# Bidirectional scan kernel: the products with B and C of both channel halves as one instruction of 2048 columns, delta u of a direction as one tile and one load

## The chip, the cores and the metric

The kernel runs on one core of a Trainium2 chip. The metric is the time of one execution in device microseconds (us). The core has five engines that work side by side, each in the order of its own queue: PE (matrix products into PSUM), DVE (vector work), ACT (activation functions and copies), POOL (vector work on SBUF alone) and SP, which here only issues transfers (DMAs). They wait for each other through semaphores. An engine that waits holds up everything behind that instruction in its queue, and SP does the same with the loads behind a load that can't be issued yet.

## What is computed

The input is eight images of 64 channels by 128 by 128, f32. The first layer runs a state-space model (Mamba) over all rows, both ways, and over all columns, both ways. Cut to one sequence and direction:

```
xz = in_w @ seq                       # 128 channels x, 128 channels z
u = silu(causal_conv(x))
dt, B, C = split(xp_w @ u)            # 4, 16 and 16 rows
delta = softplus(dt_w @ dt + dt_b)
for t:                                # per channel c and state n
    h[c, n] = exp(delta[c, t] * A[c, n]) * h[c, n] + delta[c, t] * u[c, t] * B[n, t]
    y[c, t] = sum over n of h[c, n] * C[n, t]
out = out_w @ ((y + D * u) * silu(z))
```

The mean of the four passes is group-normalized, goes through silu and is added to the input. A second layer (two 3x3 convolutions with batch norms, relu and a residual) follows.

## The kernel before

**Groups.** Four sequences of 128 points are worked on together: 512 columns. A group `n` is such a block of one image in one orientation; there are 8 x 2 x 32 = 512 groups. All of them run in one long stage; the second convolution, of some 1,300 us with the preparations at the start, comes after it.

**Units.** 128 channels by 16 states by 2 directions don't fit the 128 partitions at once. A tile holds 32 channels x 4 states on its partitions and two blocks of 32 channels side by side: 2 x 512 = 1024 columns. Such a piece of work is a unit `r`; a group has 16 (`UN`). Its `half` (r % 2) says which two of the four channel blocks; `ORDER[r]` gives the state group `ng`, the direction `d` and a kind. Two halves of the same `ng` and `d` use the same B and C, and, apart from the T units, they are neighbours in the order: (0, 1), (2, 3), (5, 6), (8, 9), (10, 11), (13, 14).

A unit goes through these steps, each a function of the kernel:

- `decay` (L421, ACT): two exponentials of 512 columns, exp(delta * A), into a PSUM tile `dA0` or `dA1` by half (for T units into an SBUF tile `s`).
- `drive` (L430): delta u times B, into an SBUF tile `s`. Units of kind V do it on DVE with B from PSUM (`pb`, made on PE by `b_rows`, L410); units of kind G on POOL with B loaded into SBUF (`bt`, by `b_tile`, L403). T units get this product from PE instead (`spread`, `turn`).
- `scan` (L453 for d = 0, L455 for d = 1, DVE): the recurrence along time, in place in `s`.
- `weigh` (L460, POOL): `s` times C (`c`, loaded by `c_rows`, L395), in place.
- `add_up` (L476, PE): for two units at a time (r, r + 1, r even), the sum over the 4 states, accumulated in the PSUM tile `yp`. This frees their `s` tiles.

Delta and delta u are written to DRAM (`dd`, L314) and loaded back with every channel on four partitions. That is `replicate` (L381): for one half and one direction it loads a tile `dl` and a tile `du`, 512 KB each.

**Order.** The order of every queue is written out by hand in the loop over `s`: step `s` is unit r of group n. In step r the loop emits, in this order: the decay of the unit after it; for a V unit the `drive` of the unit after it (so `drive(r + 1)` stands ahead of `scan(r)` on DVE); the `drive` of a G unit from `AHEAD` (r in {7, 8, 15, 0}, three units ahead, on POOL ahead of `weigh(r)`); `scan(r)`; `weigh(r)`; at r = 3 the gate of the group before (L483 on DVE, which reads the finished `yp`); the next piece of `prepare` for the group after; and at even r `add_up` of the pair four steps back (`LAG`), so (12, 13) at step 0 and (14, 15) at step 2 of the next group. At step 3 `b_rows` makes the B rows of unit 5, on PE behind the fold of (14, 15).

**Preparing the next group.** `prepare` is a generator; one piece is emitted a step. Steps 1 to 9 make z, the convolution (`cp`, L290), u, delta (softplus on ACT) and delta u (L326 on DVE, step 9), and store `dd`: first the copy `bc` of B and C (L328, ACT) goes to DRAM, then four writes of delta u and four of delta. Step 10 issues the loads of half 0, d = 0; behind them `fetch` issues c of unit 0 and `bt` of unit 2. Step 11 issues half 1, d = 0, step 13 half 1, d = 1 and step 15 half 0, d = 1.

**Buffers.** Pool `unit`: 8 tiles `s` of 1024 columns, for all kinds. Pool `rep`: five `dl`, five `du` (1024 columns each), two `bt`, five `c`. PSUM is full: `dA0`, `dA1`, `pt` (two banks each), `b` and `yp` (one each).

Of the kernel before, what the change touches and what calls it, by code (L numbers as in the profile page):

```python
# [9 lines left out]
F32 = mybir.dt.float32  # L10
# [5 lines left out]
P = 128  # L16
# [3 lines left out]
N = 512  # L20
# [4 lines left out]
NQ = 4  # L25
# [4 lines left out]
LAG = 4  # L30
# [3 lines left out]
ORDER = (  # L34
    (0, 0, "V"), (0, 0, "V"), (1, 0, "G"), (1, 0, "G"), (2, 0, "T"), (0, 1, "V"), (0, 1, "V"), (2, 0, "T"),
    (1, 1, "V"), (1, 1, "V"), (2, 1, "G"), (2, 1, "G"), (3, 0, "T"), (3, 1, "V"), (3, 1, "V"), (3, 0, "T"),
)
# [9 lines left out]
def tile_mamba2d_then_resblock(ctx: ExitStack, tc: tile.TileContext, x, par, gn, p_w, o_w, new_p, bn, cst, out):  # L47
    nc = tc.nc
# [31 lines left out]
    with tc.tile_pool(name="prep", bufs=2) as prep, tc.tile_pool(name="prep_ps", bufs=2, space=PSUM) as prep_ps:  # L80
# [4 lines left out]
        for o, p in enumerate(par):  # L85
# [8 lines left out]
            for d in range(2):  # L94
                for k in range(2):
                    for e in range(2):
                        h = slice(e * C, (e + 1) * C)
# [121 lines left out]
    with ExitStack() as st:  # L219
        big = st.enter_context(tc.tile_pool(name="big", bufs=1))  # L220
        rep = st.enter_context(tc.tile_pool(name="rep", bufs=2))
        unit = st.enter_context(tc.tile_pool(name="unit", bufs=8))
        work = st.enter_context(tc.tile_pool(name="work", bufs=2))
        small = st.enter_context(tc.tile_pool(name="small", bufs=2))
        scratch = st.enter_context(tc.tile_pool(name="scratch", bufs=2, space=DRAM))
# [48 lines left out]
        def prepare(g, before):  # L274


            w = wt[g["o"]]
            yield
            zp = psa.tile([P, N], F32, name="zp", tag="b")
            nc.tensor.matmul(  # L280
                zp.rearrange("p (q t) -> p q t", t=W), w["wz"], g["xs"][0:C, :, PAD : PAD + W], start=True, stop=True
            )
            yield
            g["sz"] = work.tile([P, N], F32, name="sz", bufs=3)
            nc.scalar.copy(g["sz"], zp)
            cp = psm.tile([P, 2, N], F32, name="cp", tag="pt")
            for d in range(2):
                for k in range(2):
                    t = PAD - 2 * k if d == 0 else PAD + 2 * k + 1
                    nc.tensor.matmul(  # L290
                        cp[:, d, :].rearrange("p (q t) -> p q t", t=W), w["wc"][:, d, k, :],
                        g["xs"][:, :, t : t + W], start=k == 0, stop=k == 1,
                    )
                yield
            yield
            u = work.tile([P, 2, N], F32, name="u")
            nc.scalar.activation(u, cp, AF.Silu, bias=w["conv_b"])  # L297
            if before is not None:
                nc.scalar.activation(before["sz"], before["sz"], AF.Silu)
            g["u"] = u  # L300
            yield
            dp = psm.tile([P, 2, N], F32, name="dp", tag="pt")
            for d in range(2):
                nc.tensor.matmul(dp[:, d, :], w["wd"], u[:, d, :], start=True, stop=True)  # L304
            yield
            yield
            nc.scalar.activation(dp, dp, AF.Softplus, bias=w["dt_b"])
            yield
            dd = g["dd"] = scratch.tile([2, 2, 32, NQ, N], F32, name="dd")

            def keep(k, v):

                for q in range(NQ):
                    nc.sync.dma_start(  # L314
                        out=dd[k, :, :, q, :].rearrange("d c t -> c d t"), in_=v[32 * q : 32 * (q + 1)]
                    )


            bp = psa.tile([P, N], F32, name="bp", tag="b")
            for d in range(2):  # L320
                nc.tensor.matmul(
                    bp[2 * NS * d : 2 * NS * (d + 1), :], w["wbc"], u[:, d, :], start=True, stop=True,
                    skip_group_check=True,
                )
            du = work.tile([P, 2, N], F32, name="du", tag="nat")
            nc.vector.tensor_mul(du, dp, u)  # L326
            bc = work.tile([4 * NS, N], F32, name="bc", tag="tok", bufs=3)
            nc.scalar.copy(bc, bp[0 : 4 * NS, :])  # L328
            bd = g["bd"] = scratch.tile([2 * NS, 2, N], F32, name="bd")
            nc.sync.dma_start(out=bd.rearrange("n d t -> d n t"), in_=bc)  # L330
            if before is not None:
                decay(before, 11)
            dl = work.tile([P, 2, N], F32, name="dl", tag="nat")
            nc.scalar.copy(dl, dp)
            for d, edge in enumerate((0, W - 1)):
                nc.scalar.copy(dl[:, d, :].rearrange("p (s t) -> p s t", t=W)[:, :, edge], far)
            keep(1, du)
            keep(0, dl)
            yield

            dt = (shared.pop("pt", None) or psm.tile([P, 2, N], F32, name="dt", tag="pt"))[:, 1, :]
            for q in range(SEQ):
                c = slice(W * q, W * (q + 1))
                nc.tensor.transpose(dt[:, c], du[:, TD, c], ident)
            replicate(g, 0, 0)
            yield
            g["duT"] = work.tile([P, SEQ, P], F32, name="duT", bufs=1)
            nc.scalar.copy(g["duT"].rearrange("p q c -> p (q c)"), dt)
            replicate(g, 1, 0)
            yield  # L350
            yield

            replicate(g, 1, 1)
            bt = psm.tile([P, 2, N], F32, name="btp", tag="pt")[:, 0, 0 : 8 * SEQ]
            for q in range(SEQ):
                nc.tensor.matmul(
                    bt[:, 8 * q : 8 * (q + 1)], u[:, TD, W * q : W * (q + 1)], w["wbc"][:, 4 * TG : 4 * TG + 8],
                    start=True, stop=True,
                )
            yield  # L360
            g["BT"] = work.tile([P, 8 * SEQ], F32, name="BT", bufs=1)
            nc.scalar.copy(g["BT"], bt)
            yield
            replicate(g, 0, 1)
            yield

        def spread(g, ng, q):
# [7 lines left out]

        def replicate(g, half, d):

            for k, what in enumerate(("dl", "du")):
                t = rep.tile([P, 2, N], F32, name=what, bufs=5)
                src = g["dd"][k, d, :, 2 * half : 2 * half + 2, :].rearrange("c q t -> c (q t)")  # L380
                nc.sync.dma_start(  # L381
                    out=t.rearrange("p q t -> p (q t)"), in_=src.unsqueeze(1).to_broadcast([32, 4, 2 * N])
                )
                g[what, half, d] = t

        def where(r):

# [10 lines left out]
        def b_tile(g, r):  # L398

            half, ng, d = where(r)  # L400
            t = rep.tile([P, N], F32, name="bt", bufs=2)
            src = g["bd"][4 * ng : 4 * ng + 4, d, :]
            nc.sync.dma_start(out=t, in_=src.partition_broadcast(32))  # L403
            g["bt", ng, d] = t
# [8 lines left out]
        def decay(g, r):  # L413

            half, ng, d = where(r)
            if ORDER[r][2] == "T":
                dA = g["s", r] = unit.tile([P, 2, N], F32, name="s")
            else:
                dA = g["dA", r] = psa.tile([P, 2, N], F32, name=f"dA{half}")
            for j in range(2):  # L420
                nc.scalar.activation(  # L421
                    dA[:, j, :], g["dl", half, d][:, j, :], AF.Exp, scale=wt[g["o"]]["A"][:, 2 * half + j, ng : ng + 1]
                )

        def drive(g, r):

            half, ng, d = where(r)
            s = unit.tile([P, 2, N], F32, name="s")
            engine, b = (nc.gpsimd, g["bt", ng, d]) if ORDER[r][2] == "G" else (nc.vector, g["pb"])
            engine.tensor_mul(s, g["du", half, d], b.unsqueeze(1).to_broadcast([P, 2, N]))  # L430
            g["s", r] = s

        def turn(g, r):

# [21 lines left out]

        def weigh(g, r):
            half, ng, d = where(r)
            s, c = g["s", r], g["c", ng, d]
            nc.gpsimd.tensor_mul(s, s, c.unsqueeze(1).to_broadcast([P, 2, N]))  # L460

        def skip(g):

# [6 lines left out]
        def add_up(g, r):  # L470

            for half in range(2):
                s = g.pop(("s", r + half))
                for j in range(2):
                    q = 2 * half + j
                    nc.tensor.matmul(  # L476
                        g["yp"][32 * q : 32 * (q + 1), :], fold, s[:, j, :], start=False, stop=r == UN - 2,
                        skip_group_check=True,
                    )
# [102 lines left out]
        UN = 4 * NG  # L582
# [9 lines left out]
            14: [(2, 0)], 15: [(2, 1), (2, 2)], 0: [(2, 3)], 1: [(3, 0)], 2: [(3, 1)], 3: [(3, 2)], 4: [(3, 3)],  # L592
        }

        AHEAD = {15: 3, 0: 3, 7: 3, 8: 3}

        ROWS = {14: 0, 3: 5, 6: 8, 9: 13}

# [6 lines left out]
        total = UN * len(gs)  # L605
# [3 lines left out]
        def at(s):  # L609
            return gs[s // UN], s % UN  # L610
# [5 lines left out]
        with tc.manual_schedule():  # L616
# [13 lines left out]
            for s in range(total + UN):  # L630
# [17 lines left out]
                    decay(*at(s + 1))  # L648
                if r in EARLY and live:
                    decay(this, EARLY[r])  # L650
                if kind == "V" and s + 1 < total:
                    drive(*at(s + 1))
                if r in AHEAD and s + AHEAD[r] < total:
                    drive(*at(s + AHEAD[r]))
# [14 lines left out]
                        spread(g, *k)  # L669
                if r == LAG and live:  # L670
                    skip(this)
                if s % 2 == 0 and LAG <= s < total + LAG:
                    add_up(*at(s - LAG))
                if r == 9 and live:
                    b_rows(this, ROWS[r])
                if r in NORM and n % PER:
# [174 lines left out]
```

## Time and profile before

| | us |
|---|---|
| median of 3 runs | 26,257.85 |
| lowest, highest | 26,257.84, 26,273.53 |
| span of the profiled execution | 26,239.0 |
| time around the span (median less span) | 18.9 |
| busy: POOL, DVE | 24,022.0, 24,018.6 |
| busy: ACT, PE | 22,246.1, 19,212.0 |
| mean busy share of the DMA engines | about 55% |

The span runs from the first to the last instruction of the profiled execution. In a line of the profile's groups stand the source line, the engine, the operation, what it writes and reads, the shape, the number of instructions; then their busy time, the mean ns of one, and the idle time of the engine just before them with what ended it. A timeline line has the start in us, the duration, the engine (SPq: SP's queue, where a transfer is issued), the line and the number of merged instructions; in brackets the idle time before it and its releaser. The records of vector instructions that follow without a gap overlap a little, so their starts stand closer than their durations.

### The profile page before, as it was taken

What the parts mean: (1) busy time and instruction counts of PE and PEld (TensorE: products, weight loads), DVE (VectorE), ACT (ScalarE), POOL (GpSimd) and SP (SyncE); (2) the same over time, 40 slices, a digit from 0 to 9 for tenths busy, and PEclk for the clock granted to TensorE, in tenths of its full rate; (3) what the DMA queues carried; (4) which work ended last, traced back from release to release, by engine and by line L of the source; (5) the groups of instructions that cost most, each with busy time, mean ns of one, the idle gap of its engine ahead of it and who ended that gap; (6) DMA issues with size and microseconds to landing.
All of it is one profiled execution on the core that took longest, in us unless ns stands there. A gap on an engine that the chain in (4) does not pass through costs nothing. (4 is left out here: it accounts for less than half of the span.)

```text
span 26239.0 us, 266043 instructions
## 1 busy us (share of the span) xinstructions
PE 19212.0 (73%) x75308; PEld 7191.5 (27%) x75308; DVE 24018.6 (92%) x14093; ACT 22246.1 (85%) x41390; POOL 24022.0 (92%) x10404
## 2 busy tenths in 40 slices
PE   6777777777777777777777777777777777777776
PEld 2222222222222223222232222222222222222232
DVE  8999999999999999999999999999999999999932
ACT  7888888888888888888888888888888888888842
POOL 7999999999999999999999999999999999999930
PEclk8888888888888888888888888888888888888888
DMA  5555555555555555555555555555555555555545
GB/s 166 173 175 171 176 186 174 178 169 174 190 171 177 169 177 189 170 176 169 184 182 175 172 176 183 177 177 171 175 185 175 175 171 177 186 172 175 172 140 190
DMA packets 2881499, 4604.73 MB, mean 175 GB/s; under 512 B 1055360, under 2 KB 1334032, under 8 KB 2864144
## 3 DMA queue, kind: packets, MB, share of 16 engines
q1 hardware_dynamic: 2859424, 4486.08, 54.9%
q10 hardware_dynamic: 15984, 68.06, 0.9%
q0 software_dynamic: 4608, 33.56, 0.3%
q8 instruction: 596, 9.76, 0.1%
q14 instruction: 887, 7.27, 0.1%
HBM read 3779.98 MB, written 738.98 MB: 172 GB/s over the span
## 5 line engine op out<-in xcount | busy, mean ns | idle before, releaser
L460 POOL TENSOR_TENSOR s<-s,c 128x1024 f32<-128x1024 f32 x8192 | 19201.7, 2372 | 983.2 <-issue 425.0
L421 ACT ACTIVATE dA<-dl,A 128x512 f32<-128x512 f32 x12288 | 8477.0, 690 | 2320.6 <-DVE s L455 1078.2
L455 DVE TENSOR_TENSOR_SCAN s<-dA,s 128x1024 f32<-128x1024 f32 x4096 | 9162.7, 2272 | 39.9 <-ACT dA L421 9.2
L430 DVE TENSOR_TENSOR s<-du,pb 128x1024 f32<-128x1024 f32 x4096 | 4930.2, 1204 | 1131.8 <-PE yp L476 556.0
L372 ACT ACTIVATE X<-duT,BT 128x128 f32<-128x128 f32 x16384 | 5603.1, 504 | 16.6
L430 POOL TENSOR_TENSOR s<-du,bt 128x1024 f32<-128x1024 f32 x2048 | 4841.3, 2364 | 154.7 <-DMA c<-bd 130.4
L410 PE MATMUL pb<-u,wb 128*128 128x512 f32 x4096 | 2776.4, 765 | 3009.8 <-ACT bc L328 2451.0
L476 PE MATMUL yp<-s,fold 128*32 128x512 f32 x32768 | 4932.0, 678 | 7.9 <-POOL s L460 7.7
L453 DVE TENSOR_TENSOR_SCAN s<-s,dA 128x1024 f32<-128x1024 f32 x2048 | 4666.1, 2278 | 52.9 <-PE dA L439 34.5
L453 DVE TENSOR_TENSOR_SCAN s<-dA,s 128x1024 f32<-128x1024 f32 x2048 | 4528.9, 2268 | 4.8 <-POOL s L430 4.1
L439 PE MATMUL dA<-ident,X 128*128 128x128 f32 x16384 | 2489.2, 301 | 783.3 <-DVE s L455 781.0
L290 PE MATMUL cp<-xs,wc 128*128 128x512 f32 x4096 | 2692.9, 792 | 140.5 <-ACT cs L572 139.7
L439 PEld LDWEIGHTS dA<-ident,X 128*128 128x128 f32 x16384 | 2034.7, 155 | 2597.1 <-DVE s L455 1892.9
L421 ACT ACTIVATE s<-dl,A 128x512 f32<-128x512 f32 x4096 | 2702.9, 707 | 0.0
L280 PE MATMUL zp<-xs,wz 64*128 64x512 f32 x1024 | 895.0, 968 | 1706.6 <-DVE s L430 1436.0
L410 PEld LDWEIGHTS pb<-u,wb 128*128 128x128 f32 x4096 | 715.2, 219 | 4487.4 <-ACT bc L328 2915.0
L476 PEld LDWEIGHTS yp<-s,fold 128*32 128x32 f32 x32768 | 824.0, 117 | 3298.8 <-issue 2282.6
L304 PE MATMUL dp<-u,wd 128*128 128x512 f32 x2048 | 1117.8, 672 | 332.7 <-ACT u L297 331.7
L421 ACT ACT_TABLE_LOAD x1030 | 1321.5, 1283 | 18.4
L290 PEld LDWEIGHTS cp<-xs,wc 128*128 128x128 f32 x4096 | 898.2, 243 | 1520.1 <-issue 969.0
L466 PE MATMUL yp<-u,dg 128*128 128x512 f32 x2048 | 961.2, 591 | 1.6 <-DVE y L483 1.6
L789 POOL DMA_DIRECT2D out<-cc x32 | 17.2, 538 | 971.9 <-ACT cc L788 971.9
(118 smaller groups left out, 13940.4 us busy)
## 6 DMA issues: line engine op xcount, KB each, us to landing
dl<-dd SPq DMA_DIRECT2D x2048, 512.0 KB
du<-dd SPq DMA_DIRECT2D x2048, 512.0 KB
c<-bd SPq DMA_DIRECT2D x4096, 256.0 KB
dd<-du SPq DMA_DIRECT2D x2048, 128.0 KB
dd<-dl SPq DMA_DIRECT2D x2048, 128.0 KB
bt<-bd SPq DMA_DIRECT2D x1024, 256.0 KB
xs<-x_h SPq DMA_DIRECT2D x512, 128.0 KB
bd<-bc SPq DMA_DIRECT2D x512, 128.0 KB
```

The costliest lines, as they stand in the source:

```text
L290: nc.tensor.matmul(cp[:, d, :].rearrange("p (q t) -> p q t", t=W), w["wc"][:, d, k, :], g["xs"][:, :, t : t + W], start=k == 0, stop=k == 1,)
L304: nc.tensor.matmul(dp[:, d, :], w["wd"], u[:, d, :], start=True, stop=True)
L372: nc.scalar.activation(t[:, :, n], g["duT"][:, q, :], AF.Copy, scale=g["BT"][:, k : k + 1])
L410: nc.tensor.matmul(pb, wt[g["o"]]["wb"][:, P * ng : P * (ng + 1)], g["u"][:, d, :], start=True, stop=True)
L421: nc.scalar.activation(dA[:, j, :], g["dl", half, d][:, j, :], AF.Exp, scale=wt[g["o"]]["A"][:, 2 * half + j, ng : ng + 1])
L430: engine.tensor_mul(s, g["du", half, d], b.unsqueeze(1).to_broadcast([P, 2, N]))
L439: nc.tensor.transpose(dB[:, j, W * q : W * (q + 1)], g["X", ng, q][:, 32 * (2 * half + j) : 32 * (2 * half + j + 1), :].rearrange("p c n - ...
L453: nc.vector.tensor_tensor_scan(s, a, b, 0.0, ALU.mult, ALU.add)
L455: nc.vector.tensor_tensor_scan(s[:, ::-1], a[:, ::-1], b[:, ::-1], 0.0, ALU.mult, ALU.add)
L460: nc.gpsimd.tensor_mul(s, s, c.unsqueeze(1).to_broadcast([P, 2, N]))
L466: nc.tensor.matmul(g["yp"], wt[g["o"]]["dg"], g["u"][:, d, :], start=d == 0, stop=False, skip_group_check=True)
L476: nc.tensor.matmul(g["yp"][32 * q : 32 * (q + 1), :], fold, s[:, j, :], start=False, stop=r == UN - 2, skip_group_check=True,)
```

## The change

- `drive` makes the product for both halves in one instruction of 4 x 512 = 2048 columns, into a tile `s2` of its own kind; the scans still run on each half (1024 columns).
- `weigh` multiplies both halves by C in one instruction, behind the scan of the second. T units keep theirs of 1024.
- `du` of a direction is one tile of 2048 columns with one load of 1 MB (`replicate_du`): d = 0 at step 10 behind `dl` of half 0, d = 1 at step 15 behind `dl` of half 0. `replicate` loads `dl` alone.
- V products are emitted once a pair, at step r where r + 1 is in `FIRST` = (0, 5, 8, 13); G products from the new `AHEAD`: that of (2, 3) of the next group at step 13 and that of (10, 11) at step 5.
- `add_up` follows the table `FOLD` (the step, and how many units back): (0, 1) at step 5, (2, 3) at 6, (4, 5) at 10, (6, 7) at 11, (8, 9) at 13, (10, 11) at 15, (12, 13) at 1 and (14, 15) at 2 of the next group.
- Buffers: four `s2` of 2048 columns and three `s` of 1024 for T units (before: eight `s`); two `du` of 2048 (five of 1024); one `bt` (two).

```diff
--- before.py
+++ after.py
@@ -219,7 +219,7 @@
     with ExitStack() as st:
         big = st.enter_context(tc.tile_pool(name="big", bufs=1))
         rep = st.enter_context(tc.tile_pool(name="rep", bufs=2))
-        unit = st.enter_context(tc.tile_pool(name="unit", bufs=8))
+        unit = st.enter_context(tc.tile_pool(name="unit", bufs=4))
         work = st.enter_context(tc.tile_pool(name="work", bufs=2))
         small = st.enter_context(tc.tile_pool(name="small", bufs=2))
         scratch = st.enter_context(tc.tile_pool(name="scratch", bufs=2, space=DRAM))
@@ -343,6 +343,7 @@
                 c = slice(W * q, W * (q + 1))
                 nc.tensor.transpose(dt[:, c], du[:, TD, c], ident)
             replicate(g, 0, 0)
+            replicate_du(g, 0)
             yield
             g["duT"] = work.tile([P, SEQ, P], F32, name="duT", bufs=1)
             nc.scalar.copy(g["duT"].rearrange("p q c -> p (q c)"), dt)
@@ -362,6 +363,7 @@
             nc.scalar.copy(g["BT"], bt)
             yield
             replicate(g, 0, 1)
+            replicate_du(g, 1)
             yield
 
         def spread(g, ng, q):
@@ -375,13 +377,19 @@
 
         def replicate(g, half, d):
 
-            for k, what in enumerate(("dl", "du")):
-                t = rep.tile([P, 2, N], F32, name=what, bufs=5)
-                src = g["dd"][k, d, :, 2 * half : 2 * half + 2, :].rearrange("c q t -> c (q t)")
-                nc.sync.dma_start(
-                    out=t.rearrange("p q t -> p (q t)"), in_=src.unsqueeze(1).to_broadcast([32, 4, 2 * N])
-                )
-                g[what, half, d] = t
+            t = g["dl", half, d] = rep.tile([P, 2, N], F32, name="dl", bufs=5)
+            src = g["dd"][0, d, :, 2 * half : 2 * half + 2, :].rearrange("c q t -> c (q t)")
+            nc.sync.dma_start(
+                out=t.rearrange("p q t -> p (q t)"), in_=src.unsqueeze(1).to_broadcast([32, 4, 2 * N])
+            )
+
+        def replicate_du(g, d):
+
+            t = g["du", d] = rep.tile([P, NQ, N], F32, name="du", bufs=2)
+            src = g["dd"][1, d].rearrange("c q t -> c (q t)")
+            nc.sync.dma_start(
+                out=t.rearrange("p q t -> p (q t)"), in_=src.unsqueeze(1).to_broadcast([32, 4, NQ * N])
+            )
 
         def where(r):
 
@@ -398,7 +406,7 @@
         def b_tile(g, r):
 
             half, ng, d = where(r)
-            t = rep.tile([P, N], F32, name="bt", bufs=2)
+            t = rep.tile([P, N], F32, name="bt", bufs=1)
             src = g["bd"][4 * ng : 4 * ng + 4, d, :]
             nc.sync.dma_start(out=t, in_=src.partition_broadcast(32))
             g["bt", ng, d] = t
@@ -414,7 +422,7 @@
 
             half, ng, d = where(r)
             if ORDER[r][2] == "T":
-                dA = g["s", r] = unit.tile([P, 2, N], F32, name="s")
+                dA = g["s", r] = unit.tile([P, 2, N], F32, name="s", bufs=3)
             else:
                 dA = g["dA", r] = psa.tile([P, 2, N], F32, name=f"dA{half}")
             for j in range(2):
@@ -425,10 +433,13 @@
         def drive(g, r):
 
             half, ng, d = where(r)
-            s = unit.tile([P, 2, N], F32, name="s")
+            s = unit.tile([P, NQ, N], F32, name="s2")
             engine, b = (nc.gpsimd, g["bt", ng, d]) if ORDER[r][2] == "G" else (nc.vector, g["pb"])
-            engine.tensor_mul(s, g["du", half, d], b.unsqueeze(1).to_broadcast([P, 2, N]))
-            g["s", r] = s
+            engine.tensor_mul(s, g["du", d], b.unsqueeze(1).to_broadcast([P, NQ, N]))
+            for k in (r, r + 1):
+                h = k % 2
+                g["s", k] = s[:, 2 * h : 2 * h + 2, :]
+            g["s2", r + 1] = s
 
         def turn(g, r):
 
@@ -456,8 +467,14 @@
 
         def weigh(g, r):
             half, ng, d = where(r)
-            s, c = g["s", r], g["c", ng, d]
-            nc.gpsimd.tensor_mul(s, s, c.unsqueeze(1).to_broadcast([P, 2, N]))
+            if ORDER[r][2] == "T":
+                s = g["s", r]
+            elif ("s2", r) in g:
+                s = g.pop(("s2", r))
+            else:
+                return
+            c = g["c", ng, d]
+            nc.gpsimd.tensor_mul(s, s, c.unsqueeze(1).to_broadcast(list(s.shape)))
 
         def skip(g):
 
@@ -592,7 +609,9 @@
             14: [(2, 0)], 15: [(2, 1), (2, 2)], 0: [(2, 3)], 1: [(3, 0)], 2: [(3, 1)], 3: [(3, 2)], 4: [(3, 3)],
         }
 
-        AHEAD = {15: 3, 0: 3, 7: 3, 8: 3}
+        AHEAD = {13: 5, 5: 5}
+        FOLD = {5: 5, 6: 4, 10: 6, 11: 5, 13: 5, 15: 5, 1: 5, 2: 4}
+        FIRST = (0, 5, 8, 13)
 
         ROWS = {14: 0, 3: 5, 6: 8, 9: 13}
 
@@ -648,7 +667,7 @@
                     decay(*at(s + 1))
                 if r in EARLY and live:
                     decay(this, EARLY[r])
-                if kind == "V" and s + 1 < total:
+                if (r + 1) % UN in FIRST and s + 1 < total:
                     drive(*at(s + 1))
                 if r in AHEAD and s + AHEAD[r] < total:
                     drive(*at(s + AHEAD[r]))
@@ -669,8 +688,8 @@
                         spread(g, *k)
                 if r == LAG and live:
                     skip(this)
-                if s % 2 == 0 and LAG <= s < total + LAG:
-                    add_up(*at(s - LAG))
+                if r in FOLD and FOLD[r] <= s < total + FOLD[r]:
+                    add_up(*at(s - FOLD[r]))
                 if r == 9 and live:
                     b_rows(this, ROWS[r])
                 if r in NORM and n % PER:
```

## The prediction

> **What bounds the kernel now.** First the busy shares and the costliest groups. They are read for two things: which engines are full, and what one instruction costs.
>
> ```profile
> PE 19212.0 (73%) x75308; PEld 7191.5 (27%) x75308; DVE 24018.6 (92%) x14093; ACT 22246.1 (85%) x41390; POOL 24022.0 (92%) x10404
> ...
> L460 POOL TENSOR_TENSOR s<-s,c 128x1024 f32<-128x1024 f32 x8192 | 19201.7, 2372 | 983.2 <-issue 425.0
> ...
> L430 DVE TENSOR_TENSOR s<-du,pb 128x1024 f32<-128x1024 f32 x4096 | 4930.2, 1204 | 1131.8 <-PE yp L476 556.0
> ...
> L430 POOL TENSOR_TENSOR s<-du,bt 128x1024 f32<-128x1024 f32 x2048 | 4841.3, 2364 | 154.7 <-DMA c<-bd 130.4
> ```
>
> POOL and DVE are equally full, and DVE's idle time stands almost wholly before L430, its product with B. The list of waits says for what:
>
> ```profile
> DVE s L430 <- PE yp L476: 556.0, 574, 3.8
> DVE s L430 <- DMA du<-dd: 528.5, 570, 14.3
> ```
>
> So about once a group DVE waits for a fold that frees an s buffer, and once for the load of delta u. The timeline of one group shows the loop that closes there. Time is counted from the end of the scan of unit 7 (17.72 + 2.28 = 20.00 after 20,000), called zero below.
>
> ```profile
> 20017.72 2.28 DVE L453 TENSOR_TENSOR_SCAN s<-s,dA 128x1024 f32<-128x1024 f32 x1
> ...
> 20026.51 0.57 ACT L328 COPY bc<-bp 64x512 f32<-64x512 f32 x1
> ...
> 20035.22 0.54 SPq L381 DMA_DIRECT2D dl<-dd  x1
> ...
> 20037.10 0.60 SPq L403 DMA_DIRECT2D bt<-bd  x1
> ...
> 20043.51 2.35 POOL L430 TENSOR_TENSOR s<-du,bt 128x1024 f32<-128x1024 f32 x1
> ...
> 20045.82 2.36 POOL L460 TENSOR_TENSOR s<-s,c 128x1024 f32<-128x1024 f32 x1
> 20046.28 1.22 DVE L430 TENSOR_TENSOR s<-du,pb 128x1024 f32<-128x1024 f32 x1 [1.87 <-DMA du<-dd]
> ```
>
> From unit 7's scan, ACT's softplus work leads to the copy of bc (end 7.1), SP then writes dd and issues the loads (dl half 0 at 15.2), and the first product of the next group that needs du half 1 starts at 26.3. Over 502 groups of the trace the copy ends at 7.1 (7.09 to 7.16 from the 10th to the 90th percentile), so this chain is rigid, and that product starts at 26.0. DVE then needs 22.8 to the next unit 7; 26.0 + 22.8 is the 48.83 us that I find between successive L326 instructions. **This loop (zero, loads, DVE, zero) is the bound**; POOL, at about 47, follows close behind. The execution is 26,239.0: 511 distances of 48.83 are 24,952, and 1,287 lie outside. The median run is 18.9 above the span.
>
> **What is saved.** Where instructions follow without a gap, starts on POOL are 2.32 apart for L460 and 1.22 for the 128x512 addition L528. Another 512 columns thus cost 1.10, and 2048 columns 2.32 + 2.20 = 4.52 against 4.64 for two. Per group six products with C and two with B merge on POOL: 8 x 0.12 = 0.96. On DVE L430 starts are 1.12 apart and L483 with 512 columns 0.58, so 2048 columns cost 2.20 against 2.24; four merges give 0.16. The row of L787, 2048 columns on DVE at 2351 ns busy, bounds this price from above. The saving is POOL's, and POOL isn't the bound. The Trainium skill (GPSIMD Engine Reference, 3.1 Elementwise) gives 4497 ns for a tensor_tensor of 2048 f32 columns, where the rows here (2372 ns, and 1268 ns for 512 columns) make 2372 + 2 x 1104 = 4580 busy; by the page the chain below would be 0.17 us a group shorter, some 85 in all.
>
> **What moves.** Three things, per group:
>
> (1) *Delta u half 1 is loaded sooner, and needed sooner.* The packets' records give these mean ends: dl half 0 at 18.3, du half 0 at 20.8, bt at 21.9, dl half 1 at 23.3, du half 1 at 25.0. The moved bytes of that window, per 0.75 us from 20,030 on:
>
> ```profile
> GB/s 128 161 213 306 249 249 169 5 0 339 202 382 404 366 320 150 306 317 388 407 410 423 410 412 412 432 415 388 404 359 239 208 169 129 33 90 246 14 0 0
> ```
>
> So 512 KB take 1.67 once the queue is full, and the consumer starts 1.0 after the last packet. In the new order du is one load behind dl half 0: 18.3 + 2 x 1.67 = 21.6, usable at 22.6. But its DVE product now stands ahead of the scan of unit 15, not behind it. DVE reaches it at 19.9: scans 8, 9 (4.4), L326 (1.1), a wait to 6.65 for the decay of unit 10 (ACT gives it just before the bc copy, of 0.57, starts), scans 10, 11 (4.4), the product of 13 (2.2), scans 12 to 14 (6.6). So DVE waits 2.7 instead of 0.9. The old 0.93 wait for a fold before the product of 13 (second position after scan 11) goes, and is swallowed by this one.
>
> (2) *POOL's product with B for units 2 and 3 is moved ahead of the products with C of 13, 14 and 15* (AHEAD from 15: 3 to 13: 5). It needs bt of the next group, which SP issues behind dl half 0, the whole of du and c0. These are 0.5 + 1.0 + 0.25 + 0.25 MB = 2.1 MB, exactly what now lies ahead of the end of dl half 1, so bt's last packet is at 23.3 and it is usable at 24.3. POOL has finished unit 12 by about 18 (below). It stands in order, so it **idles some 6 us, and the C products of 13/14 and 15 queue behind**: 24.3 + 4.52 + 4.52 = 33.34 (13/14 done), + 2.32 = 35.66 (15 done; before, POOL finished it at 28.2 in the rows above).
>
> (3) *Who waits for those.* PE's order is written out: the fold of (12, 13) at step 1, the conv product cp at step 2, the fold of (14, 15), then at step 3 pb for unit 5. The DVE gate L483 waits for the last fold, and the DVE product for 5 and 6 for pb. From 33.34: 0.1 to start, fold 1.07 (eight records of L476 in this timeline), cp 1.99 (four of L290 in the group at 13,017; 3.69 in this one, with PE's weight loads 0.34 instead of 0.19), fold 1.07, pb 1.12 (L410), 0.1: DVE starts that product at 38.8. Without this wait it would be there at 22.6 + 2.2 + five scans at 2.2 + gate 0.6 = 36.4. Then 2.2 + scans 4 to 6 (6.6) + 2.2 + scan 7 (2.28) = 13.3. **The new distance is 38.8 + 13.3 = 52.1.**
>
> Check on POOL: from 35.66, units 0/1 to 40.2, 2/3 to 44.7, 4 to 47.0, B of 10/11 to 51.5, that is -0.6 in the next group; 5/6 to 3.9, 7 to 6.3, 8/9 to 10.8, 10/11 to 15.3, 12 to about 18. So it does stand ready long before 24.3.
>
> *Cost nothing by this walk:* bt with one buffer instead of two: its old reader, the B product of 10/11, ends at -0.6, and the new load is issued at 17; without these 17 us of cover every us that POOL lags more would be paid. The Trainium skill (Trainium Kernel Development and Optimization, Best Practices) asks for double buffers so that loads and work overlap, and so speaks against this; the issue at 17.1 shows the overlap kept, and by the rule some of bt's 1 us would be added. Also the four s2 buffers (each reused fold lies at least 3 us back), SP's c load of unit 13 (waits for 5/6 at 3.9; bd is due at 7.1), and ACT (its continuous run of decays and X between scan 0 and scan 6 is 13.1 against 13.8 of DVE). One load issue less in two is about 0.6 of SP, which isn't late.
>
> **Sum.** 52.1 - 48.83 = 3.25 (unrounded); x 511 = 1,661; 26,239 + 1,661 + 19 = **27,920**. Ends: if the queue ran at 410 GB/s, as in the burst's later slices, the 1.57 MB behind dl half 0 would take 3.8 instead of 5.0, so 1.2 a group less: 27,300. If cp always took 3.69, 1.7 more: 28,790; PE's granted clock over the trace is 0.847, so I take a third of it, 28,210, and half of the lag of SP below on top: 28,500.
>
> **Rivals.** *Only the du load decides* (POOL's products of 14, 15 not late enough, or PE not held): 22.6 + 27.1 = 49.7, +0.8 a group: 26,690. For it: the wait for du is in the list already. Against: the 6 us between POOL ready and bt. 14%.
>
> *Faster, the merged instructions count.* If neither load binds, DVE's spaced work is the next floor: 48.83 less its waits of about 2.4 is 46.4, less 0.16 is 46.2; POOL about 46. With 1 us of remaining waits, 47.2, or -1.6 a group: 25,420. One thing decides it: bt must be usable before 48.83 - (52.1 - 24.3) = 21.0, not 24.3, and du before 21.7. That needs 1.57 MB in 1.7 us behind dl half 0; no slice in the burst passes 432 GB/s. It remains for a queue order other than the one I read. 13%.
>
> *Worse.* POOL's lag blocks SP: x1's write waits for POOL in a quarter of the groups, and the c loads in all; if bd starts 1.5 later in every group the distance is 53.6: 28,690. 8%.
>
> *The change doesn't do what it says* (the load of half 1 isn't needed earlier since the tile framework splits it): no more than 0.2% either way, 3%.
>
> **Numbers.** Forecast 62%, own range 27,300 to 28,500. The range 26,600 to 28,700 takes in the du rival and half of the worse one, and leaves out the faster one. What can be told from no change is about 0.2%, or 53 us. Faster 13%, same 3%, slower 84%.
>
> **What would show it.** Right: a gap on POOL of 4 to 7 us before L430, released by the bt load; a gap on DVE before the gate L483 (released by PE's yp) or the product behind it of 2 to 3 us, where all 512 together wait 7.5 us now; a gap before the first product released by du of 2 to 3; L326 distances near 52. POOL's busy time falls by 8 x 0.164 (2 x 2372 less 4580 ns) x 512, some 670 us, while the span grows. Wrong: POOL without that gap, or bt landing at 21 or sooner; then the walk's order of loads is false. If the gap is there but the gate doesn't wait, the step through PE is false, and the time is that of the du rival.

## The result, and the profile after

| | before | after |
|---|---|---|
| median of 4 runs, us | 26,257.85 | 28,919.85 |
| lowest, highest | 26,254.96, 26,273.53 | 28,910.66, 28,929.12 |
| span of the profiled execution | 26,239.0 | 28,927.3 |
| mean distance between the scans of unit 7 | 48.82 | 54.05 |
| mean granted clock of TensorE | 0.847 | 0.812 |

The changed kernel is **slower by a tenth**: ratio 1.1008, interval 1.0992 to 1.1023. I had forecast 27,920: the sign was right, the size too small by 1,000 us, and the time lies above the range. 511 distances of 54.05 are 27,620, and 1,307 lie outside them (1,291 before, by the same measure); so the loss is in the groups, 5.23 us in each.

The busy shares and costliest groups of the changed kernel, the lines that answer to those of before:

```profile
PE 19901.2 (69%) x75308; PEld 7280.4 (25%) x75308; DVE 24040.4 (83%) x12045; ACT 22313.5 (77%) x41390; POOL 23399.6 (81%) x6308
...
L438 POOL TENSOR_TENSOR s<-du,bt 128x2048 f32<-128x2048 f32 x1024 | 4656.0, 4547 | 3217.9 <-DMA bt<-bd 2902.9
...
L438 DVE TENSOR_TENSOR s<-du,pb 128x2048 f32<-128x2048 f32 x2048 | 4659.0, 2275 | 1375.2 <-DMA du<-dd 800.2
```

POOL's work shrank by 622 us in 4,096 fewer instructions, and DVE's not at all (22 us more); POOL now stands still for a fifth of the span and DVE for a sixth. What they stand still for is in the list of waits of the changed kernel (total us, times, longest):

```profile
POOL s L438 <- DMA bt<-bd: 2902.9, 479, 7.6
PE yp L493 <- POOL s L477: 2497.5, 508, 7.5
...
DVE y L500 <- PE yp L493: 1424.2, 461, 5.2
...
DVE s L466 <- ACT dA L429: 816.4, 765, 1.6
DVE s L438 <- DMA du<-dd: 800.2, 297, 14.6
```

The first three lines are one chain: POOL waits for bt once a group (some 6 us), PE then for POOL's product with C, and DVE's gate for PE's fold. Before, the gate waited 7.5 us in all. The timeline of one group of the changed kernel shows it in order of time. Its zero, the end of the scan of unit 7, is 20,010.81.

```profile
20008.53 2.28 DVE L464 TENSOR_TENSOR_SCAN s<-s,dA 128x1024 f32<-128x1024 f32 x1
...
20017.49 4.47 DVE L466 TENSOR_TENSOR_SCAN s<-dA,s 128x1024 f32<-128x1024 f32 x2 [1.21 <-ACT dA L429]
...
20034.58 2.29 DVE L438 TENSOR_TENSOR s<-du,pb 128x2048 f32<-128x2048 f32 x1 [2.30 <-PE pb L418]
20035.95 4.53 POOL L438 TENSOR_TENSOR s<-du,bt 128x2048 f32<-128x2048 f32 x1 [6.99 <-DMA bt<-bd]
...
20040.44 15.87 POOL L477 TENSOR_TENSOR s<-s,c 128x2048 f32<-128x2048 f32 x4
...
20045.03 1.92 PE L493 MATMUL yp<-s,fold 128*32 128x512 f32 x4 [5.97 <-POOL s L477]
...
20046.88 3.23 PE L290 MATMUL cp<-xs,wc 128*128 128x512 f32 x4
...
20050.04 1.07 PE L493 MATMUL yp<-s,fold 128*32 128x512 f32 x8
...
20051.03 1.12 PE L418 MATMUL pb<-u,wb 128*128 128x512 f32 x2
20051.20 0.69 DVE L500 TENSOR_TENSOR y<-yp,sz 128x512 f32<-128x512 f32 x1 [3.29 <-PE yp L493]
...
20052.20 2.29 DVE L438 TENSOR_TENSOR s<-du,pb 128x2048 f32<-128x2048 f32 x1 [0.31 <-PE pb L418]
```

POOL idles 6.99 for bt; the product with C of 13/14 starts at 20,040.44 (29.6 after zero) and ends 4.5 later; PE, idle for 5.97, folds unit 13 and makes cp, and only then comes the fold of (14, 15), for which the gate has waited 3.29. New to the forecast are two durations on PE: after its idle time four records of the fold take 1.92, and cp takes 3.23; the next fold and pb run in 1.07 and 1.12 again.

The same in means over 500 groups, us after zero, with the walk of the prediction beside it:

| | forecast | measured |
|---|---|---|
| POOL's B product of 2/3 starts | 24.3 | 24.24 |
| POOL idle before it | some 6 | 6.05 |
| DVE's product of 0/1 starts | 22.6 | 23.36 |
| PE starts the fold of unit 13 | 33.44 | 33.42 |
| cp starts | 34.5 | 35.26 |
| cp takes | 1.99 | 3.42 |
| fold of (14, 15) ends | 37.6 | 39.73 |
| DVE's product of 5/6 starts | 38.8 | 40.9 |
| distance | 52.1 | 54.05 |

Along the chain from bt over POOL to PE's fold the walk holds within 0.1 us; DVE's product of 0/1 came 0.8 late, which costs nothing here, since the gate waits 3 us later on. **The whole miss of 2 us arises between 33.4 and 39.7, on PE**, and 13.2 from the product of 5/6 to the next zero is again as forecast (13.3).

### The profile page after: what moved, and what is told of

It reads as the page before. It is cut to its first block, busy times and chain, and to the rows that moved or that the text cites. A ratio compares the mean times of both kernels' runs of the same rounds, so it can differ in the third digit from the quotient of the medians.

```text
span 28927.3 us, 254788 instructions
## 1 busy us (share of the span) xinstructions
PE 19901.2 (69%) x75308; PEld 7280.4 (25%) x75308; DVE 24040.4 (83%) x12045; ACT 22313.5 (77%) x41390; POOL 23399.6 (81%) x6308
## 5 line engine op out<-in xcount | busy, mean ns | idle before, releaser
L477 POOL TENSOR_TENSOR s<-s,c 128x2048 f32<-128x2048 f32 (+1 forms) x5120 | 18641.8, 3667 | 1219.5 <-issue 720.9
L493 PE MATMUL yp<-s,fold 128*32 128x512 f32 x32768 | 5973.5, 708 | 2497.5 <-POOL s L477 2497.5
L438 POOL TENSOR_TENSOR s<-du,bt 128x2048 f32<-128x2048 f32 x1024 | 4656.0, 4547 | 3217.9 <-DMA bt<-bd 2902.9
L418 PE MATMUL pb<-u,wb 128*128 128x512 f32 x4096 | 2996.5, 821 | 4155.0 <-ACT bc L328 4144.6
L438 DVE TENSOR_TENSOR s<-du,pb 128x2048 f32<-128x2048 f32 x2048 | 4659.0, 2275 | 1375.2 <-DMA du<-dd 800.2
L450 PE MATMUL dA<-ident,X 128*128 128x128 f32 x16384 | 2361.9, 291 | 217.4 <-DVE s L466 212.0
L500 DVE TENSOR_TENSOR y<-yp,sz 128x512 f32<-128x512 f32 x512 | 354.1, 692 | 1566.9 <-PE yp L493 1424.2
L280 PE MATMUL zp<-xs,wz 64*128 64x512 f32 x1024 | 675.4, 743 | 817.9 <-DVE s L438 722.0
L304 PE MATMUL dp<-u,wd 128*128 128x512 f32 x2048 | 1020.5, 621 | 312.5 <-ACT u L297 312.5
L357 PE MATMUL btp<-xpT,u 128*128 128x8 f32 x4096 | 657.6, 288 | 508.3 <-ACT xp L523 329.3
```

Source lines behind the costliest of these rows:

```text
L280: nc.tensor.matmul(zp.rearrange("p (q t) -> p q t", t=W), w["wz"], g["xs"][0:C, :, PAD : PAD + W], start=True, stop=True)
L418: nc.tensor.matmul(pb, wt[g["o"]]["wb"][:, P * ng : P * (ng + 1)], g["u"][:, d, :], start=True, stop=True)
L438: engine.tensor_mul(s, g["du", d], b.unsqueeze(1).to_broadcast([P, NQ, N]))
L450: nc.tensor.transpose(dB[:, j, W * q : W * (q + 1)], g["X", ng, q][:, 32 * (2 * half + j) : 32 * (2 * half + j + 1), :].rearrange("p c n - ...
L477: nc.gpsimd.tensor_mul(s, s, c.unsqueeze(1).to_broadcast(list(s.shape)))
L493: nc.tensor.matmul(g["yp"][32 * q : 32 * (q + 1), :], fold, s[:, j, :], start=False, stop=r == UN - 2, skip_group_check=True,)
```

## Experiments: the chain from bt over POOL to PE

**Undo the move on POOL.** The product of 2/3 goes back to step 15, behind the products with C of 13/14 that it held up; all else is as in the changed kernel.

```diff
-        AHEAD = {13: 5, 5: 5}
+        AHEAD = {15: 3, 5: 5}
```

> The kernel after with one entry changed: POOL's product with B for units 2 and 3 of the next group is issued at step 15, behind the product with C of 13/14, instead of at step 13 ahead of it. Theory (the chain bt load, POOL's queue, PE's queue, gate): 13/14 no longer waits for bt, 15 ends at 24.3 + 4.5 + 2.3 = 31.1 instead of 35.7, the gate waits no more, and what is left is the loop through the load of du: 23.4 + 27.1 = 50.5 us between groups, 27,100 us in all. Rival 1 (DVE's own waits set the loop, for du 2.4 and for the decay of unit 10 1.2, and the gate's wait is only slack): no change, 28,900. Rival 2 (the 2048-column pieces are too coarse, wherever they stand): above 28,500.

Measured: 27,273.24, ratio 1.0387 (1.0371 to 1.0402), distance 50.83. DVE's waits in this kernel:

```profile
DVE s L466 <- ACT dA L429: 814.4, 764, 1.6
DVE s L438 <- DMA du<-dd: 693.3, 265, 15.5
```

The gate's wait for yp, 1,424 us in the changed kernel, is down to 8, and POOL's gap before the B product of 2/3 fell from 6.05 to 0.05 a group. On top of the rest of the change the move costs 28,920 less 27,273, so **1,647 us, 62% of the loss**. The other 1,010 us belong to the rest of the change. What is left waiting: 1.88 a group before the product of 0/1, 1.21 before scan 10, 0.51 before scan 12, 0.39 before scan 14. The first of these has two causes: in the row groups du ends it (2.5 a group), in the column groups mostly pb on PE (1.2), as in the changed kernel (2.8 and 2.0).

**Leave the move and take cp out of the way**: the fold of (12, 13) goes to step 2, behind cp, so that cp runs while PE would wait.

```diff
-        FOLD = {5: 5, 6: 4, 10: 6, 11: 5, 13: 5, 15: 5, 1: 5, 2: 4}
+        FOLD = {5: 5, 6: 4, 10: 6, 11: 5, 13: 5, 15: 5, 2: 4}
...
+                if r == 2 and 6 <= s < total + 6:
+                    add_up(*at(s - 6))
```

> The kernel after with PE's fold of (12, 13) moved from step 1 to step 2, behind the conv product cp; nothing else. Theory: cp runs before POOL has finished 13/14, so the wait costs only two folds and pb behind 35.7: the gate starts 2 to 3.5 us sooner, 50.7 to 52.1 us between groups, 27,200 to 27,900 us. If PE's queue is not in the chain: 28,900, no change.

Measured: 28,072.38, ratio 1.069 (1.0674 to 1.0706), distance 52.37. The right direction, with less effect than expected. The gate's wait fell from 3.06 to 0.80, but the product behind it now waits 0.70 for pb: the folds end at 37.64, since unit 15's product with C is late too (35.7 by the prediction's walk), and pb stands behind them.

**Leave the order and keep PE busy.** Five f32 products with the identity, whose result nobody reads, stand ahead of the fold of (12, 13); nothing of the computation is left out. In the timeline below each is two records.

```diff
+                if r == 1 and live and n:
+                    wp = psm.tile([P, 2, N], F32, name="wp", tag="pt")
+                    for k in range(5):
+                        nc.tensor.matmul(wp[:, 0, :], ident, this["u"][:, 0, :], start=True, stop=True)
```

> The kernel after with five more f32 matrix products of 512 columns per group into a PSUM tile that nobody reads, on PE just ahead of the fold of (12, 13), where PE stands idle for some 6 us. Theory: PE's granted clock is 0.5 in the stretch after that idle time, so that fold and cp take 1.9 and 3.4 us; with work in the idle time it is granted 1.0, they take 1.1 and 2.0, and the distance falls by about 2 us to 52: 27,900 us. Rival (the slow clock has nothing to do with PE's idling): no gain, or up to 1.5 us a group more, 28,900 to 29,700.

Measured: 28,406.88, ratio 1.0816 (1.0798 to 1.0834), distance 53.04, half of the gain expected. By kind of group, the column groups went from 53.83 to 51.56 and the row groups without a convolution from 54.04 to 51.60. The row groups in which a piece of the second layer's convolution or norm is emitted went up, from 54.41 to 55.59. The loss is in the convolution's 18 of 64 groups (54.06 to 55.83; of the rest all but the first of an image gained): there the idle products wait for the PSUM tile `pt` that this work holds, until ACT has copied it out (502 us in 112 waits). So the products were left out in the convolution's groups:

```diff
-                if r == 1 and live and n:
+                if r == 1 and live and n and not 6 <= n % PER < 24:
```

> As warm, but the five idle products are left out in the 18 of 64 groups in which the first convolution holds the PSUM tile that they use (there warm lost 1.2 us a group, in all others it won 2.3). Theory: 46 groups at 51.6 and 18 at 54.3 us, mean 52.3, 28,000 us. Rival (the loss lies elsewhere): 28,300 or more.

Measured: 28,137.34, ratio 1.0712 (1.0696 to 1.0728), distance 52.51; column groups 51.53, row groups without a convolution 51.58, the others 54.17. The timeline of a group with the idle products (zero is 18,879.67):

```profile
18904.30 4.54 POOL L438 TENSOR_TENSOR s<-du,bt 128x2048 f32<-128x2048 f32 x1 [6.48 <-DMA bt<-bd]
...
18906.99 4.56 PE L694 MATMUL wp<-u,ident 128*128 128x512 f32 x10
...
18911.49 1.05 PE L493 MATMUL yp<-s,fold 128*32 128x512 f32 x4
...
18913.40 1.05 PE L493 MATMUL yp<-s,fold 128*32 128x512 f32 x4 [0.87 <-POOL s L477]
...
18914.39 1.99 PE L290 MATMUL cp<-xs,wc 128*128 128x512 f32 x4
...
18916.31 1.06 PE L493 MATMUL yp<-s,fold 128*32 128x512 f32 x8
...
18917.47 0.69 DVE L500 TENSOR_TENSOR y<-yp,sz 128x512 f32<-128x512 f32 x1 [0.74 <-PE yp L493]
```

POOL waits for bt as before (6.48), and the fold and cp read and write the same data in the same order, but they take 1.05 and 1.99 instead of 1.92 and 3.23. The view by windows says why. First the six us of the changed kernel's group from PE's idle time to the fold, and the six behind it; then the second six for the group with idle products (PE, PEld, DVE, ACT and POOL busy, granted clock, DMA share, GB/s):

```profile
20039.00:20045.00 6.00, 0.06 (x2) 0.00 (x0) 6.00 (x4) 5.80 (x14) 6.00 (x3) 0.80 0.43 178
20045.00:20051.00 6.00, 5.97 (x16) 1.52 (x16) 2.90 (x2) 5.97 (x15) 6.00 (x2) 0.63 0.47 119
```

```profile
18912.00:18918.00 6.00, 5.13 (x22) 1.41 (x19) 5.25 (x4) 5.97 (x16) 6.00 (x3) 1.00 0.22 80
```

PE does nothing for 6 us, and the clock granted in the 6 us behind that is 0.63; where it was kept at work the clock there is 1.00. That settles the 2 us: it is **the clock after an idle PE**, on average 4.9 us idle in the changed kernel.

## Experiments: the parts by themselves

**One load of delta u, nothing else.** The kernel before with `replicate_du` as in the change; B products in halves, the old order.

```diff
+            replicate_du(g, 0)
...
-            engine.tensor_mul(s, g["du", half, d], b.unsqueeze(1).to_broadcast([P, 2, N]))
+            engine.tensor_mul(s, g["du", d][:, 2 * half : 2 * half + 2, :], b.unsqueeze(1).to_broadcast([P, 2, N]))
```

> The kernel before with one part of the change alone: du of a direction as one tile of 2048 columns with one load of 1 MB; the products stay in halves, in their old order. Theory (the loop through the load of du): both halves are usable at 23.4 us after the scan of unit 7 instead of 20.8 + 1.0 and 26.0; the product of unit 0 (at 21.7 before) waits 1.7 us, and that of unit 1 comes at 23.4 + 1.1 + 2.2 = 26.7 instead of 26.0: 49.5 us between groups, 26,600 us. Rival (half as many loads relieve SP and the DMA queue): 26,000 or less.

Measured: 26,269.03, ratio 1.0002 (0.9993 to 1.0011). My expectation was wrong; the load by itself costs nothing and saves nothing. DVE's waits in this kernel:

```profile
DVE s L438 <- PE yp L484: 592.6, 599, 2.4
...
DVE s L438 <- DMA du<-dd: 546.3, 424, 15.6
```

The two totals are close to those of before (556.0 and 528.5). The wait has only moved: the gap before the product of unit 0 grew from 0.24 to 1.17 a group, that before unit 1 fell from 0.88 to nothing, and unit 1's product started at 26.04 as it had at 26.00.

**The merged products with C alone.** The kernel before with `s2` tiles and one `weigh` for both halves; B products in halves, two loads of du; to make room du has four buffers and bt one. `weigh` is that of the change.

```diff
+            if r + 1 < UN and ORDER[r] == ORDER[r + 1] and ("s2", r) not in g:
+                s2 = g["s2", r + 1] = unit.tile([P, NQ, N], F32, name="s2")
+            else:
+                s2 = g["s2", r]
+            s = s2[:, 2 * half : 2 * half + 2, :]
```

> The kernel before with another part of the change alone: the products with C merged to 2048 columns (six a group), everything else in halves as before. To make room, du has four buffers instead of five and bt one instead of two. Theory (POOL is not the bound before the change, the load of du is): POOL's busy time falls by about 500 us, and the time stays within 0.3% of before. Rival (POOL is the bound): 6 x 0.12 = 0.7 us a group less, 25,890 us.

Measured: 26,443.44, ratio 1.0067 (1.0052 to 1.0082), so worse than I allowed. The loss stands in one kind of group: those in which POOL adds x1 (`xr`) went from 49.23 to 50.48, the others from 48.70 to 48.81. Fewer buffers of du and bt came with the merged products here, and no run tells the two apart.

**Undo more from the changed kernel's side.** On top of the move undone, DVE's product of 0/1 goes behind scan 15; then in addition the load of du is issued ahead of `dl`'s.

```diff
-        FIRST = (0, 5, 8, 13)
+        FIRST = (5, 8, 13)
...
+                if r == 0 and live and s:
+                    drive(this, 0)
```

> The kernel of pool15 (POOL's product of units 2/3 at step 15) and DVE's product of units 0/1 moved behind the scan of unit 15, to step 0. Theory (what is left is the loop through du): DVE needs du 2.2 us later and waits some 0.5 us for it; 23.4 + 24.9 = 48.3 us between groups, 25,950 us. Rival (DVE's work and ACT's decays are the floor, not du): as pool15, within 0.5%.

Measured: 26,875.1, ratio 1.0232 (1.0217 to 1.0247), well above what I expected. The wait for du is nearly gone (164 us), and the row groups without a convolution came down from 49.8 to 48.1; but the wait of 1.21 before scan 10 stays, and in the column groups, at 51.1, scan 15 waits 2.10 for `turn` on PE.

```diff
-            replicate(g, 0, 0)
             replicate_du(g, 0)
+            replicate(g, 0, 0)
```

> As pool15_v0, and the load of du (d = 0) is issued ahead of that of dl of half 0 instead of behind it. Theory: du is usable 2 us sooner, at 21.4, and no product waits for it; what is left is DVE's own work and waits on ACT, 46.2 + 1 to 1.5 = 47.2 to 47.7 us between groups, 25,400 to 25,700 us. Rival (dl of half 0, now 3.3 us later, is late for the decay of unit 0): 26,200 or more.

Measured: 26,830.52, ratio 1.0216 (1.0201 to 1.0231). A miss: du no longer decided anything, and the two waits that did are untouched. Some 570 us over the kernel before remain. Why PE's `turn` is late in the column groups I have not settled by a run. The trace of the kernel above shows where: their output takes a second product on PE, `btp` starts at 18.5 us after zero against 16.1 in the row groups without a convolution, the clock granted from 20 to 22 is 0.50 against 1.00, and `turn` starts at 23.0 against 19.0. Their median distance is 51.2 in this kernel, in the one above and in the first experiment.

## Experiments: towards a faster kernel

**The old order, with the parts that cost nothing.** The kernel before with merged C products and one load of du, that of d = 0 issued ahead of `dl`; B products in halves where they were, bt with one buffer.

```diff
+            replicate_du(g, 0)
             replicate(g, 0, 0)
```

> The kernel before with merged products with C and du as one tile and load, that load issued ahead of dl of half 0; the products with B stay in halves, in the old order. Theory: du is usable at 21.4, as the product of unit 0 asks for it at 21.7, so nothing waits for du: 48.8 less 0.9 for du, less some of the 0.9 before the product of unit 13, 47.2 to 48.0 us between groups, 25,400 to 25,850 us. Rival (POOL takes over as the bound at its 46.4): not below 46.8, 25,200; or dl late for the decays: 26,200 or more.

Measured: 26,046.51, ratio 0.9914 (0.9898 to 0.9931): faster, by less than I hoped. What waits most now is scan 12 (0.96 a group), whose `turn` on PE stands behind a fold of (6, 7) that waits for the merged product:

```profile
DVE s L465 <- PE dA L451: 482.6, 480, 1.9
```

So this fold was moved one step, from 10 to 11, behind that `turn`:

```diff
-                if s % 2 == 0 and LAG <= s < total + LAG:
-                    add_up(*at(s - LAG))
+                late = 5 if r == 11 else LAG
+                if (s % 2 == 0 and r != 10 or r == 11) and late <= s < total + late:
+                    add_up(*at(s - late))
```

> As b_both_duf, with PE's fold of (6, 7) moved from step 10 to step 11, behind the transposes that the scan of unit 12 waits for. Theory: the 0.96 us a group that DVE waits before that scan falls to about 0.1, nothing else stands ready to take its place: 48.4 - 0.9 = 47.5 to 47.7 us between groups, 25,570 to 25,670 us. Rival (POOL, at 46.6 busy, or the load of du takes over): 25,900 or more.

Measured: **25,859.17, ratio 0.9845 (0.983 to 0.986)**, the best kernel of this study, faster than before and after. Scan 12's wait is gone, and the time is some 200 us above the expected one: waits of 0.16 to 0.37 a group are left before scans 14, 1, 2 and 3, all but that of scan 3 hardly there before. On this one the two merged B products were put back singly.

**With DVE's B products merged**, at the places of the change:

```diff
+            if ORDER[r][2] == "V":
+                engine.tensor_mul(s2, g["du", d], b.unsqueeze(1).to_broadcast([P, NQ, N]))
...
-                if kind == "V" and s + 1 < total:
+                if (r + 1) % UN in (0, 5, 8, 13) and s + 1 < total:
```

> As b_both_fold11, and DVE's products with B merged to 2048 columns, at the steps of the change (each ahead of the scan of the unit before its pair). Theory: the merge saves 0.16 us a group and costs more, since the product of unit 9 no longer stands between the scans of 7 and 8 while ACT works through softplus: the scan of unit 10 waits 1.2 us; in column groups the scan of 15 or 14 waits too. 1.0 to 1.8 us a group over b_both_fold11, 26,100 to 26,500 us. Rival (only POOL's order did harm): as b_both_fold11 or 0.2 us a group less, 25,500.

Measured: 26,166.12, ratio 0.9962 (0.9947 to 0.9977): 307 us slower than without, as expected. The wait for ACT's decay before scan 10, first without and then with the merged products:

```profile
DVE s L467 <- ACT dA L429: 135.6, 276, 0.8
```

```profile
DVE s L473 <- ACT dA L429: 694.0, 652, 1.6
```

In halves, unit 9's product stands behind scan 7, and covers 1.12 us of ACT's softplus work before decay 10. Merged, it stands ahead of scan 7, and the wait a group rises from 0.09 to 1.21: by 1.12, just that product. DVE's busy time fell by 169 us, and the kernel still grew by 307.

**With POOL's B products merged**, at steps 15 and 7:

```diff
+            if ORDER[r][2] == "G":
+                engine.tensor_mul(s2, g["du", d], b.unsqueeze(1).to_broadcast([P, NQ, N]))
...
-        AHEAD = {15: 3, 0: 3, 7: 3, 8: 3}
+        AHEAD = {15: 3, 7: 3}
```

> As b_both_fold11, and POOL's products with B merged to 2048 columns, at steps 15 (behind the product with C of 13 and 14) and 7. Theory: POOL isn't the bound, so its 0.24 us a group bring nothing; unit 15's product with C comes 2.2 us later, and PE's fold of (14, 15) at step 2 still doesn't wait: within 0.4% of b_both_fold11. Rival (POOL is the bound now): 25,450 us.

Measured: 26,113.55, ratio 0.9941 (0.9925 to 0.9958), 254 us slower than without, where I had expected no difference. All of it is in the groups with an `xr` addition: 48.82 became 51.08, the others stayed at 47.86 and 47.85. In this kernel SP's 128 waits for that addition, before x1 is written, are 2,032 us together, against 1,674 without the merged products, so 2.8 us longer each, and DVE's waits for du rose from 58 to 336 us. That fits a load of du that is queued behind the write; no run took that wait away alone.

## Why the forecast was right in sign and too small

**Right.** The loop through bt, POOL, PE and the gate is what the change puts in place of the old one. Putting POOL's product back took 1,647 us away. Most of the signs that I had named are there: POOL's gap of 6.05 released by bt (4 to 7), the gate's 3.06 (2 to 3), and 2.37 before the product of 0/1 (2 to 3), though du ends it in the row groups only (249 of 256) and in most column groups pb does (204 of 255). The distance, 54.05 and not near 52, is the one that failed. POOL's saving of 622 us (670 forecast) buys nothing, since POOL isn't the bound.

**The step that failed is (3), PE's order, in the durations "fold 1.07, cp 1.99".** Both were read from stretches in which the clock was full. Measured are 33.42 to 35.26 for the fold and 3.42 for cp, 2.2 us more together than forecast. The steps behind gave 0.2 back, and 2 x 511 is the missing 1,000 us. The records of the granted clock, averaged over 490 groups, show it: 0.50 from 33 to 36 us after zero, 0.59 to 0.73 from 36 to 39, 0.99 from 40 on. The idle products in all groups brought the clock from 33 to 38 up to 0.87 to 0.95, cp to 2.01, and the column groups and the row groups without a convolution to 51.5 to 51.6, where I had forecast 52.1. So the mechanism and the rest of the sum stand; the term on PE was mis-sized.

The trace of before could have told me. Over its groups cp took 3.36 on average and 1.99 only in one group of seven; I had both 1.99 and 3.69 in view and chose 1.99 as the rule. Where cp was slow there, PE's longest idle time in the 9 us ahead of it was 3.9 us on average, where it was fast 0.8. The mean alone gives 52.1 + 1.4 and some 28,600, inside the range. And for the range I weighed 3.69 with the clock over the whole trace, 0.847; the clock where cp runs, 28 to 32 us after zero, was 0.62 to 0.67. I had put PE's wait into the walk myself, and didn't ask what an idle PE does to the work that follows it.

The Trainium skill has the rule (TensorE: Matmul & The Clock Gate, Part 1: The HAM clock gate): the array's clock is gated to half after an idle window of about 3.4 us, and is full again after as long at work. The trace agrees on the drop: in the group shown above the clock's record goes to 0.5 some 3.5 us into PE's idle time. It is full again 4.4 us after the fold's start there, and some 6 us on average over the groups, longer than that figure. The page calls the ramp less than 1% of a typical kernel's span, and speaks there of the start of a kernel; here it comes once a group, and the idle products won back 783 us of 28,920, 2.7%, net of their own cost.

**The du rival** ("only the du load decides", 49.7 a group and 26,690) is what the first experiment made: 50.83 and 27,273. It was 583 us too low. The first product starts at 23.4, not 22.6, and in the column groups it was mostly pb on PE that released it last (in the group of the changed kernel shown above pb took 2.08 us, not 1.12). From there to the next zero it is 27.4, not 27.1. So du alone doesn't decide in that kernel either.

**ACT at no cost** was right only under this cover. I had seen DVE wait to 6.65 for decay 10 and let the du wait swallow it. It is 1.21 a group in the changed kernel and costs nothing there, since the gate waits later anyway; the experiment with merged DVE products shows that it costs time as soon as the later waits are gone.

**The other rivals.** SP's lag ("worse") didn't come: SP's c loads wait longer for POOL (12,642 us against 7,190), but the copy bc ended at 7.09 (7.11 before), bd was issued at 7.15 (7.14), and bt's product started at 24.24. The faster side didn't come by the merged instructions: a merged product saves 0.08 us of busy time on DVE (169 us over 2,048, in the experiment with DVE's B products merged) and 0.15 on POOL (622 over 4,096), but it stands where the earlier of its halves stood, needs all of its inputs there, and gives its result where the later half did.

Left open: how much of the column groups' wait for `turn`, where the product of 0/1 stands behind scan 15, is the clock's doing, and by how much the x1 write delays du. A version with two bt buffers, or with bt loaded ahead of du, wasn't tried.

## What to carry to other kernels

Before two instructions are merged, ask what each half covered and what waited for the first half: in an in-order queue the merged one waits for the latest input and releases at the latest output, and a tenth of a us saved can cost several. A duration taken from a row is only as good as the state in which it was measured: look at the granted clock in the place where the instruction will run, and if the new walk idles PE ahead of it (4.9 us on average here), take the half-clock row. Undo parts singly and jointly, since a wait that costs nothing under another (1.21 before scan 10) becomes the price once that other is removed.

## What the runs showed of the hardware

Idle products of 4.56 us ahead of a PE chain on the critical path gained 783 us net (28,920 to 28,137), though nobody reads what they make; but a PSUM tile that other work holds turned the gain into a loss of 1.8 us in the groups that shared it (54.06 to 55.83).

A 1 MB load in place of two of 512 KB in this queue changed nothing that can be measured (1.0002, 0.9993 to 1.0011).

The granted clock's records are 0.5 or 1.0 and come in multiples of 3.413 us, and the column groups of three kernels settled at a median distance of 51.2, which is 15 times that. That the one holds the other is not shown; no run separated them.
